# First attention of a two-layer transformer: the correction product in four column strips, and a block's normalization factors on GpSimd

## The chip, the cores and the metric

The kernel runs on one core of a Trainium2 chip. The metric is the device time of one execution in microseconds (us), as the median of several runs. The engines of the core work side by side, each through its own queue in order: TensorE (PE in the profile; its weight loads are PEld), VectorE (DVE), ScalarE (ACT), GpSimd (POOL), and SyncE (SP), which issues most transfers.

## The reference

An image tokenizer gives 128 images of 64 tokens with 256 features. Two layers follow, each with an attention and a feed-forward part, both behind a layer norm and added to the stream. Only the first attention of layer 0 is touched:

```python
h = h + _L0_attn_ref(_layernorm(h), Wq, Wk, Wv, w_mlp, b_mlp)

# in _L0_attn_ref: 8 groups g of 32 features d
Q, K, V = x @ Wq.T, x @ Wk.T, x @ Wv.T
diff = Q[b, q, g, d] - K[b, k, g, d]              # for every pair of tokens q, k
attn = relu(einsum('bqkgd,d->bqkg', relu(diff), w_mlp) + b_mlp[0])
attn = softmax(attn, axis=k)
out  = einsum('bqkg,bkdg->bqdg', attn, V)

# _layernorm(h): (h - mean) / sqrt(var + 1e-5), over the 256 features
```

There is no product of Q and K here: for every pair of tokens and every feature a rectified difference is formed, and only the weighting with `w_mlp` is a matrix product. So VectorE, GpSimd and ScalarE do the elementwise work and TensorE the sums.

## The kernel before

The program has stages one after another: the tokenizer (to about 186 us), the first attention (to about 1102 us), the expert attention of layer 0, the linear attention of layer 1, and the routed experts. The stream `h2` stays in on-chip memory, all in float32.

**Blocks and chunks.** `relu_attention` takes the 128 images in 8 blocks of 16 (`NB`). A block's pairs of query and key are done in 8 chunks of 8 query tokens each, so there are 64 chunks. One chunk's scores lie in one PSUM tile `sc` of 128 partitions (16 images by 8 groups) by 8 queries by 64 keys.

**A chunk's elementwise parts.** For each image `i` and half `hf` of the features a part of 128 x 512 is formed, in one of three ways: `larger` (L530, VectorE) writes max(q, k) in place of relu(q - k), which differs from it by k; `difference` (L538, GpSimd, then L539, ScalarE) writes relu(q - k); `by_query` (L548, ScalarE) does the same for single images. `add` brings the parts of four images into `sc` with `summed` (L340): four products with 32 columns of weights each, which write partitions 0, 32, 64 and 96 onwards. Such four are called a quad here.

**The correction.** Since `larger` gives max(q, k) = relu(q - k) + k, the weighted sum of the keys has to be taken off again. `key_sums` and `correction` (L454) put it, with the bias, into `kb` (128 x 64), once in a block. `begin` spreads it over the 8 queries of a chunk as the first product into `sc` (L525): identity times `kb`, repeated eight times along the free axis.

**The scores after that.** `less_max` (L564 to L566, VectorE), `exponents` (L571, ScalarE), `sums` (L574, L575, VectorE), `weights` (L578, GpSimd), `transpose` (L587, TensorE) and `transposed` (L595, ScalarE) form the softmax of chunk n within chunk n + 1.

**The order.** The order of each engine is written out by hand under `tc.manual_schedule()`. In a chunk TensorE takes six quads of `add`, of which `add(4, 1)` is the last, then the next chunk's `begin`, then the old chunk's `transpose`, and then `add(12, 0)` and `add(12, 1)`, which end the chunk's scores. Steps of the neighbouring blocks are hung into named places of a chunk by the table `work`: "W" lies behind `weights`, ahead of the last differences; "V1" and "V2" lie among VectorE's maxima.

**The factors of a block.** Each block needs its layer norm. `statistics` (L360, L361, VectorE) gives mean and variance for each of 8 tiles (`mv`), `factors` the reciprocal root: L370 adds the epsilon on VectorE, L371 takes the power on GpSimd, both at "W". One chunk later, at "V1", `offsets` (L375, VectorE) multiplies the mean by the factor and by -1. `normal` (L388, ScalarE; L386, VectorE, in the first block alone) applies factor and offset, and transposes and the products for keys, values and queries follow (L397, L409, L428, L463). From block 3 on, four tiles are done at chunk n - 17 and four at n - 13, where n is the block's first chunk.

Of the kernel before, what the change touches and what calls it, by code (L numbers as in the profile page):

```python
# [15 lines left out]
ALU = mybir.AluOpType  # L16
# [4 lines left out]
P = 128  # L21
# [3 lines left out]
LN_EPS = 1e-5  # L25
# [34 lines left out]
def bcast(ap, axis, n):  # L60

    v = ap.unsqueeze(axis)
    shape = list(v.shape)
    shape[axis] = n
    return v.to_broadcast(shape)
# [241 lines left out]
def relu_attention(c, sh, wqkv, wmlp, bmlp, beside):  # L307
# [6 lines left out]
    tc, nc, h2 = c.tc, c.nc, c.h2  # L314
    NB = 16
    NP = NB // 2
    np_, bp, atp, ep = sh.np_, sh.bp, sh.atp, sh.ep
    with (
# [29 lines left out]
        class Block:  # L348
# [14 lines left out]
            def factors(self, i0=0, i1=NP):  # L363

                if i0 == 0:
                    self.rs = np_.tile([P, NP], F32, tag="rs", name="rs")
                    self.nb = np_.tile([P, NP], F32, tag="nb", name="nb")
                i = slice(i0, i1)
                rs = self.rs[:, i]
                nc.vector.tensor_scalar_add(rs, self.mv[:, i, 1], LN_EPS)  # L370
                nc.gpsimd.tensor_tensor(rs, rs, c.nhalf[:, i], ALU.pow)  # L371

            def offsets(self, i0=0, i1=NP):
                i = slice(i0, i1)
                nc.vector.scalar_tensor_tensor(  # L375
                    self.nb[:, i], self.mv[:, i, 0], -1.0, self.rs[:, i], ALU.mult, ALU.mult
                )

            def normal(self, n, vector=False):
                if n == 0:  # L380
# [133 lines left out]
        class Chunk:  # L514
# [7 lines left out]

            def begin(self):
                self.sc = pss.tile([P, 8, T], F32, tag="sc", name="sc")
                nc.tensor.matmul(self.sc, c.ident, bcast(self.blk.kb, 1, 8), start=True, stop=False)  # L525

            def larger(self, pool, i, n, hf):
                m = pool.tile([P, n, 8, T], F32, tag="m", name="m")
# [72 lines left out]
        def at(n, place, *steps):  # L601
            work.setdefault((n, place), []).extend(steps)

        def of(f, *a):
            return lambda: f(*a)

        def first(x):

            for half in range(2):
                for n in range(4 * half, 4 * half + 4):  # L610
                    x.statistics(n)
                x.factors(4 * half, 4 * half + 4)
            for half in range(2):
                x.offsets(4 * half, 4 * half + 4)
            for n in range(4):
                x.normal(n)
                x.normal(4 + n, True)
            for i in (0, 2, 1, 3):
                x.transpose(i)
                x.transposed(i, i > 1)  # L620
            for s in range(2):
                x.keys(s, 0)
                x.keyed(s, 0, s == 1)
            x.queries(0)
            x.queried(0)
# [8 lines left out]
        for b, x in enumerate(blocks):  # L634
            n = 8 * b

            if b + 1 < len(blocks):
                at(n + 9, "X", of(x.outcome, 0))
                at(n + 9, "A", of(x.outcome_copied, 0, 0))
                at(n + 9, "B", of(x.outcome_copied, 0, 1))  # L640
                at(n + 9, "Y", of(x.outcome, 1))
                at(n + 9, "C", of(x.outcome_copied, 1, 0))
                at(n + 10, "O", of(x.outcome_copied, 1, 1))
                for i in range(4):
                    at(n + 10 + i // 2, "XY"[i % 2], of(x.back, i))
                    at(n + 10 + (i + 1) // 2, ("V2", "V1")[i % 2], of(x.added, i))
            if b == 0:
                for i in range(4):
                    at(i // 2 * 2, "XY"[i % 2], of(x.values, i))
                    at(i // 2 * 2, "AB"[i % 2], of(x.valued, i))  # L650
                continue

            if b == 1:
                at(0, "V1", *(of(x.statistics, i) for i in range(NP)))
                at(0, "W", x.factors)
                at(0, "V2", x.offsets)
                at(0, "C", of(x.normal, 0), of(x.normal, 1))
                at(1, "X", of(x.transpose, 0))
                at(1, "A", of(x.normal, 2), of(x.transposed, 0))
                at(1, "B", of(x.normal, 3))  # L660
                at(1, "Z", of(x.transpose, 1))
                at(2, "O", of(x.transposed, 1))
            else:
                for i in range(NP):
                    at(n - 21 + i if b > 2 else 1 + i // 4, "V2", of(x.statistics, i))
                at(n - 17 if b > 2 else 2, "W", of(x.factors, 0, 4))
                at(n - 16 if b > 2 else 3, "V1", of(x.offsets, 0, 4))
                at(n - 13, "W", of(x.factors, 4, 8))
                at(n - 12, "V1", of(x.offsets, 4, 8))
                for i in range(4):  # L670
                    at(n - 12 + i, "C", of(x.normal, i))
                at(n - 8, "X", of(x.transpose, 0))
                at(n - 8, "A", of(x.transposed, 0))
                at(n - 8, "Z", of(x.transpose, 1))
                at(n - 7, "O", of(x.transposed, 1))
            for i in range(2):
                at(n - 6 + i, "A", of(x.normal, 4 + 2 * i))
                at(n - 6 + i, "B", of(x.normal, 5 + 2 * i))
                at(n - 6 + i, "Z", of(x.transpose, 2 + i))
                at(n - 5 + i, "O", of(x.transposed, 2 + i))  # L680
            for fo in range(2):
                at(n - 4 + fo, "X", of(x.keys, 0, fo))
                at(n - 4 + fo, "A", of(x.keyed, 0, fo))
                at(n - 4 + fo, "Z", of(x.keys, 1, fo))
                at(n - 3 + fo, "O", of(x.keyed, 1, fo))
            at(n - 2, "X", of(x.values, 0))
            at(n - 2, "A", of(x.valued, 0))
            at(n - 2, "Y", x.key_sums)
            at(n - 1, "V1", x.correction)
            at(n - 1, "X", of(x.values, 1))  # L690
            at(n - 1, "A", of(x.valued, 1))
            at(n - 1, "Z", of(x.values, 2))
            at(n, "O", of(x.valued, 2))
            at(n, "Y", of(x.values, 3))
            at(n, "B", of(x.valued, 3))
# [8 lines left out]
        with tc.manual_schedule():  # L704
            seq = [(x, q0) for x in blocks for q0 in range(0, T, 8)]
            first(blocks[0])
            ch, old = Chunk(*seq[0]), None
            for n in range(len(seq)):
# [1460 lines left out]
@with_exitstack  # L2169
def vit_tower(ctx: ExitStack, tc: tile.TileContext, a, out):  # L2170
    const = ctx.enter_context(tc.tile_pool(name="const", bufs=1))
    dram = ctx.enter_context(tc.tile_pool(name="dram", bufs=1, space=DRAM))
    c = Ctx(tc, const)

    hd = dram.tile([B, T, D], F32, name="hd")

    hx = dram.tile([B, T, D], F32, name="hx")
    gfd = dram.tile([B * T, 1], F32, name="gfd")
    with tc.tile_pool(name="stream", bufs=1) as sp:
        c.h2 = sp.tile([P, B // 2, D], F32, name="h2")  # L2180
        tokenizer(c, a["x"], a["w1"], a["bn1"], a["w2"], a["bn2"])
        with ExitStack() as rings:
            sh = Shared(c, rings)
            beside, rest = expert_attention(
                c, sh, hd, *(a[k] for k in ("normw", "wr", "br", "wqkvf", "wvf", "wproj", "bproj", "wout"))
            )
            rest(*relu_attention(c, sh, a["wqkv0"], a["wmlp"], a["bmlp"], beside))
    c.tables(ctx.enter_context(tc.tile_pool(name="tables", bufs=1)))
    with tc.tile_pool(name="gate", bufs=1) as gp:
        k = Routing(c, gp, a["wg"], a["bg"])  # L2190
        linear_attention(c, hd, hx, out, k, a["wqk1"], a["bqk1"], a["wv1"], a["bv1"], a["wg"])
        experts(c, hx, gfd, out, a["we1"], a["we2"], a["be2"], lambda: route(c, k, gfd))
# [71 lines left out]
```

## Time and profile before

| What | Value |
|---|---|
| Median of 3 runs | 2685.99 us (2681.73 to 2687.66) |
| The profiled execution | 2687.57 us |
| Its span, first to last instruction | 2685.8 us |
| First attention, in the span | 196 to 1102 us |
| L525, begin: records, between | 128, 201.7 and 1082.9 us |
| L340 into `sc`: records, mean | 4096, 598 ns |
| L375: count, shortest, median, longest | 15; 156, 930, 1866 ns |
| L370: count, median | 15; 118 ns |
| L371: count, median | 15; 1009 ns |
| Granted TensorE clock, mean | 0.981 |

A line of the profile names engine, source line, operation, the tile written and those read, the shape, the count and times. One product in float32 appears as two records of TensorE, so 64 products of `begin` are 128 records. Matmuls are pipelined[...]; how long a product holds the engine is read from the starts of the lines that follow each other. "[0.34 <-DVE m L530]" says that the engine stood idle for 0.34 us and that VectorE's L530 ended the wait.

### The profile page before, as it was taken

Reading aid. Unit: us, or ns where it says so; the run is one execution under the profiler, and the core shown is the slowest. Engines: PE = TensorE matmul, PEld = TensorE weight load, DVE = VectorE, ACT = ScalarE, POOL = GpSimd, SP = SyncE. Lnnn points to the kernel's source line nnn. Section 1 sums busy time; section 2 is a strip of 40 time slices with the busy share of each in tenths; the row PEclk is TensorE's granted clock in tenths of the full one; section 3 lists DMA queues with packets and bytes.
Section 4 is the critical chain, followed back from the end, with each engine's and each line's share of the span. In section 5 each row is a group of like instructions: output and inputs, shape, how many; then the busy total and the mean of one; then the engine's idle time right before and its main releaser. Section 6 shows DMA issues by size and latency. Waiting matters only on the chain.

```text
span 2685.8 us, 80910 instructions
## 1 busy us (share of the span) xinstructions
PE 2539.0 (95%) x35229; PEld 1724.6 (64%) x35229; DVE 2024.2 (75%) x3028; ACT 1624.6 (60%) x3421; POOL 1618.6 (60%) x1381
## 2 busy tenths in 40 slices
PE   8989999999999999899999999999799987999997
PEld 4553444444444444688888888888466565888886
DVE  5759999999999989878877888877367786444443
ACT  2228888888888988766666666665245533332332
POOL 3318889888898998566666666653232312445544
PEclk9999999999999999999999999999899998999998
DMA  3100000000000000000000000000435454555554
GB/s 111 32 13 1 2 2 2 1 2 1 2 2 1 2 12 2 3 12 19 11 11 19 12 19 12 11 19 11 118 64 126 95 123 151 177 193 191 197 186 134
DMA packets 138271, 141.14 MB, mean 53 GB/s; under 512 B 107875, under 2 KB 121701, under 8 KB 130224
## 3 DMA queue, kind: packets, MB, share of 16 engines
q1 hardware_dynamic: 127536, 118.40, 14.8%
q0 software_dynamic: 7648, 14.77, 1.7%
q8 instruction: 278, 4.55, 0.7%
q10 hardware_dynamic: 2720, 2.69, 0.3%
q14 instruction: 89, 0.73, 0.1%
HBM read 104.03 MB, written 32.54 MB: 51 GB/s over the span
## 4 chain that ended last, share of the span: by engine, by line
PE 71%; DVE 18%; issue 4%; ACT 4%; POOL 1%; DMA 1%; DVEq 0%; POOLq 0%; SPq 0%; ACTq 0%
PE sc L340 12%; PE po L2108 6%; DVE m L530 6%; PE ph L2092 6%; PE pc L184 5%; PE pt L1102 4%; PE pqk L1019 4%; PE sc L1066 4%; PE pq L1426 4%; PE pv L1041 3%; PE pz L1115 3%; PE pt L587 2%; PE sc L525 2%; PE pv L1440 2%; PE pk L409 2%
## 5 line engine op out<-in xcount | busy, mean ns | idle before, releaser
L538 POOL TENSOR_TENSOR m<-q,k 128x1024 f32<-128x1024 f32 x384 | 720.1, 1906 | 69.3 <-PE sc L340 56.3
L530 DVE TENSOR_TENSOR m<-pc,k 128x2048 f32<-128x2048 f32 (+1 forms) x320 | 647.2, 2058 | 0.5 <-ACT q L474 0.5
L340 PE MATMUL sc<-m,wide 128*32 128x512 f32 x4096 | 517.3, 598 | 13.9 <-DVE m L530 7.9
L539 ACT ACTIVATE m<-m 128x1024 f32<-128x1024 f32 x384 | 403.0, 1050 | 11.1 <-POOL m L538 10.5
L340 PEld LDWEIGHTS sc<-m,wide 128*32 128x32 f32 x4096 | 127.8, 109 | 281.4 <-issue 165.7
L548 ACT ACTIVATE m<-k,q 128x64 f32<-128x64 f32 x1024 | 271.0, 340 | 0.9 <-DVE k L421 0.9
L1078 DVE TENSOR_REDUCE mx<-sc 128x16 f32<-128x1024 f32 x128 | 156.1, 1220 | 135.3 <-PE sc L1066 135.3
L1093 POOL TENSOR_TENSOR e<-e,mx 128x1024 f32<-128x1024 f32 x128 | 243.6, 1903 | 10.0
L1025 ACT COPY kr<-pqk 128x512 f32<-128x512 f32 x254 | 137.7, 603 | 140.4 <-PE pqk L1019 140.4
L2092 PE MATMUL ph<-xt,w1s 128*128 128x256 f32 x896 | 198.9, 380 | 3.6 <-DVE xt L2083 2.7
L2108 PE MATMUL po<-w2s,hT 128*128 128x256 f32 x896 | 198.0, 379 | 0.0
L1092 POOL TENSOR_TENSOR mx<-mx,gate 128x16 f32<-128x16 f32 x128 | 27.7, 216 | 278.9 <-ACT z L1123 152.7
L2092 PEld LDWEIGHTS ph<-xt,w1s 128*128 128x128 f32 x896 | 169.8, 190 | 28.3 <-DVE xt L2083 3.3
L2108 PEld LDWEIGHTS po<-w2s,hT 128*128 128x128 f32 x896 | 168.1, 190 | 21.7
L1105 ACT COPY pT<-pt 128x512 f32<-128x512 f32 x256 | 139.0, 598 | 50.4 <-PE pt L1102 50.0
L1079 DVE TENSOR_TENSOR e<-sc,mx 128x1024 f32<-128x1024 f32 x128 | 156.7, 1225 | 4.4
L2126 POOL DMA_INDIRECT out<-y,rout x56 | 56.8, 1013 | 167.7 <-ACT hT L2096 124.8
L1085 DVE TENSOR_REDUCE mx<-e 128x16 f32<-128x1024 f32 x128 | 152.5, 1191 | 4.0 <-ACT e L1082 3.8
L1102 PE MATMUL pt<-ident,e 128*128 128x128 f32 x1024 | 143.1, 282 | 9.5 <-DVE vr L1055 6.3
L2096 ACT ACTIVATE hT<-ph,w1s 128x256 f32<-128x256 f32 x224 | 93.2, 471 | 96.8 <-PE ph L2092 96.8
L2113 ACT ACTIVATE y<-y,gf 128x256 f32<-128x256 f32 x56 | 28.0, 507 | 196.4 <-issue 107.3
L1082 ACT ACTIVATE e<-e 128x1024 f32<-128x1024 f32 x128 | 139.5, 1090 | 2.2 <-DVE e L1079 1.9
(330 smaller groups left out, 5013.6 us busy)
## 6 DMA issues: line engine op xcount, KB each, us to landing
w1s<-in_we SPq DMA_DIRECT2D x30, 1028.0 KB, 5.2
w2s<-in_we SPq DMA_DIRECT2D x30, 1024.0 KB, 4.9
hd<-h SPq DMA_DIRECT2D x16, 512.0 KB, 3.4
x<-hd SPq DMA_DIRECT2D x16, 512.0 KB, 3.9
h<-hd SPq DMA_DIRECT2D x4, 2048.0 KB, 12.8
hx<-h SPq DMA_DIRECT2D x4, 2048.0 KB, 11.8
out<-h SPq DMA_DIRECT2D x4, 2048.0 KB, 20.6
xt<-in_x SPq DMA_DIRECT2D x15, 512.0 KB, 3.6
```

The source lines that it names most:

```text
L340: nc.tensor.matmul(dst[j : j + 32], wide[:, hf, s : s + 32], part, start=start, stop=stop)
L530: nc.vector.tensor_tensor(m, bcast(self.pq[:, hf, i : i + n], 3, T), k, ALU.max)
L538: nc.gpsimd.tensor_tensor(m, bcast(self.q[:, hf, s : s + 2], 3, T), k, ALU.subtract)
L539: nc.scalar.activation(m, m, AF.Relu)
L548: nc.scalar.activation(self.parts[i, hf][:, q], self.blk.k[:, hf, i], AF.Relu, bias=self.q[:, hf, i - NB // 2, q : q + 1], scale=-1.0,)
L1078: nc.vector.tensor_reduce(mx, sc, AX.X, ALU.max)
L1079: nc.vector.tensor_sub(e, sc, bcast(mx, 2, T))
L1085: nc.vector.tensor_reduce(self.sm[x], self.e[x], AX.X, ALU.add)
L1093: nc.gpsimd.tensor_mul(e, e, bcast(sm, 2, T))
L1102: nc.tensor.transpose(pt[:, cq, :], e[:, i : i + 2, :].rearrange("p e s -> p (e s)"), c.ident)
L2092: nc.tensor.matmul(ph[:, j], self.w1[:, w0 : w0 + P], self.xt[:, fc], start=(fc == 0), stop=(fc == 1))
L2108: nc.tensor.matmul(po, self.hT[:, f, r * P : r * P + P], self.w2[:, f, :], start=(f == 0), stop=(f == 7))
```

## The change

`begin` forms the same sum in four products: 32 columns of the identity at a time, each into its 32 partitions of `sc`, with the same moving operand. `factors` does all its steps on GpSimd: the epsilon, the power, and then the offset in two steps, mean times factor and times -1. `offsets` and its places in the table are gone, so the offsets are formed at "W", one chunk before, and in the first block half by half. What is computed stays the same.

```diff
@@ factors, offsets
-                nc.vector.tensor_scalar_add(rs, self.mv[:, i, 1], LN_EPS)
+                nc.gpsimd.tensor_scalar_add(rs, self.mv[:, i, 1], LN_EPS)
                 nc.gpsimd.tensor_tensor(rs, rs, c.nhalf[:, i], ALU.pow)
-
-            def offsets(self, i0=0, i1=NP):
-                i = slice(i0, i1)
-                nc.vector.scalar_tensor_tensor(
-                    self.nb[:, i], self.mv[:, i, 0], -1.0, self.rs[:, i], ALU.mult, ALU.mult
-                )
+                nc.gpsimd.tensor_mul(self.nb[:, i], self.mv[:, i, 0], rs)
+                nc.gpsimd.tensor_scalar(self.nb[:, i], self.nb[:, i], -1.0, None, ALU.mult)
@@ begin
-                nc.tensor.matmul(self.sc, c.ident, bcast(self.blk.kb, 1, 8), start=True, stop=False)
+                for j in range(0, P, 32):
+                    j = slice(j, j + 32)
+                    nc.tensor.matmul(
+                        self.sc[j], c.ident[:, j], bcast(self.blk.kb, 1, 8), start=True, stop=False
+                    )
@@ first
-            for half in range(2):
-                x.offsets(4 * half, 4 * half + 4)
@@ the table of steps
                 at(0, "W", x.factors)
-                at(0, "V2", x.offsets)
...
                 at(n - 17 if b > 2 else 2, "W", of(x.factors, 0, 4))
-                at(n - 16 if b > 2 else 3, "V1", of(x.offsets, 0, 4))
                 at(n - 13, "W", of(x.factors, 4, 8))
-                at(n - 12, "V1", of(x.offsets, 4, 8))
```

## The prediction

> **What bounds the kernel now.** I read the page first, then the stretches of the span, then the chain of waits, and then the order of time around the two places that change. The profiled execution took 2687.57 us, span 2685.8; it lies 1.6 above the median of the runs, 2685.99.
>
> ```profile
> PE 2539.0 (95%) x35229; PEld 1724.6 (64%) x35229; DVE 2024.2 (75%) x3028; ACT 1624.6 (60%) x3421; POOL 1618.6 (60%) x1381
> ...
> PE 71%; DVE 18%; issue 4%; ACT 4%; POOL 1%; DMA 1%; DVEq 0%; POOLq 0%; SPq 0%; ACTq 0%
> ```
>
> TensorE (PE) carries the span, VectorE (DVE) the rest. The change lies in the first attention, 196 to 1102 us; its stretch (busy us of PE, PEld, DVE, ACT and POOL, with instructions; then clock, DMA share, GB/s), and the chain in it by line:
>
> ```profile
> 196.00:1102.00 906.00, 891.42 (x9599) 392.51 (x9598) 851.15 (x849) 788.74 (x1781) 804.39 (x486) 1.00 0.01 2
> ```
> ```profile
> by line: PE sc L340 35.4%; DVE m L530 17.8%; PE pt L587 6.4%; PE sc L525 6.1%; PE pk L409 5.0%; PE pc L463 4.9%; PE pv L428 4.8%; PE po L484 2.2%; DVE e L566 1.8%; DVE pc L564 1.8%; ACT m L539 1.7%; DVE mx L574 1.5%; DVE nb L375 1.4%; DVE h
> ```
>
> PE is busy 98% and DVE 94%, and the chain goes to and fro between them. Both lines that change stand in it: PE L525 with 6.1% of 906 = 55.3 us, DVE L375 with 1.4% = 12.7 us. GpSimd (POOL) is busy 89% but hardly in the chain.
>
> PE in order of time (start, duration, count of records; each fp32 product has two records). Starts tell more than durations, which overlap:
>
> ```profile
> 606.61 1.07 PE L340 MATMUL sc<-m,wide 128*32 128x512 f32 x8 [0.32 <-DVE m L530]
> 607.61 1.13 PE L525 MATMUL sc<-kb,ident 128*128 128x512 f32 x2
> 608.66 1.15 PE L587 MATMUL pt<-ident,e 128*64 128x64 f32 x32
> 609.75 1.98 PE L409 MATMUL pk<-xT,w 128*128 128x512 f32 x4
> ...
> 626.10 2.78 PE L340 MATMUL sc<-m,wide 128*32 128x512 f32 x24
> 628.81 1.99 PE L428 MATMUL pv<-w,xT 128*128 128x256 f32 x8
> ```
>
> One quad of column strips (8 records) takes 607.61 - 606.61 = 1.00 us to the next line, three quads (24) take 628.81 - 626.10 = 2.71. So a further quad costs (2.71 - 1.00)/2 = 0.857, and leaving the strip shape 0.14. The full-array product L525 takes 608.66 - 607.61 = 1.05; four such records (L409, next line at 611.66) take 1.91, so a product costs 0.86 and leaving the full shape 0.20. **A quad costs what one full product costs; the rest is the price of changing shape.**
>
> **What the Trainium skill says.** TensorEngine Tiling (Array Packing), Key Properties: a change of tiling mode, not of the tile alone, drains TensorE, and different tiles run in parallel. The trace agrees: 0.14 and 0.20 at changes, and four strips in the time of one product. SBUF — State Buffer, Who interferes with whom: a DVE instruction with two SBUF inputs contends with a GpSimd instruction that reads SBUF, and the later one blocks fully. The trace agrees at L375 (inputs `mv` and `rs`): 0.16 us at the start, where POOL is idle, but 0.93 as median:
>
> ```profile
> L375 DVE SCALAR_TENSOR_TENSOR nb<-mv,rs x15: 156/930/1866, 186.3 to 826.2; 128x4 f32<-128x4 f32 x14, 128x8 f32<-128x8 f32 x1
> ```
>
> **Part 1, begin.** One 128-column product becomes four 32-column ones. They follow `add(4, 1)`, which is in the strip shape already, so quad, begin, leave costs 2 x 0.857 + 0.14 = 1.85 where it was 1.00 + 1.05 = 2.05. Gain 0.197 us for each of 64 chunks. The first product keeps the wait of L525 (for `kb`, or for the strips before); the other three have none. On the chain stand 55.3 / 1.055 = 52 of 64: **52 x 0.197 = 10.2 us**. The other 12 lie where DVE is late anyway; nothing there. Unshown: that four strips may read the same moving operand (`kb`) at full rate; in L340 each strip has its own. Bounds: -12.6 (all 64 count) to the rival below; I take 10.2.
>
> **Part 2, DVE's steps go.** L370 (15, 0.12 us) and L375 leave DVE; between 196 and 1102 there are 13 of each. L370 adds 0.03 from start to start: 0.3 us in all. L375 comes twice in a block of eight chunks:
>
> ```profile
> 432.58 1.36 DVE L375 SCALAR_TENSOR_TENSOR nb<-mv,rs 128x4 f32<-128x4 f32 x1
> 433.87 2.28 DVE L530 TENSOR_TENSOR m<-pc,k 128x2048 f32<-128x2048 f32 x1
> ...
> 488.43 0.53 DVE L375 SCALAR_TENSOR_TENSOR nb<-mv,rs 128x4 f32<-128x4 f32 x1
> 488.88 2.28 DVE L530 TENSOR_TENSOR m<-pc,k 128x2048 f32<-128x2048 f32 x1
> ```
> ```profile
> 436.92 1.92 PE L340 MATMUL sc<-m,wide 128*32 128x512 f32 x16
> 439.18 1.07 PE L340 MATMUL sc<-m,wide 128*32 128x512 f32 x8 [0.34 <-DVE m L530]
> ...
> 491.00 2.87 PE L340 MATMUL sc<-m,wide 128*32 128x512 f32 x16
> 494.19 1.06 PE L340 MATMUL sc<-m,wide 128*32 128x512 f32 x8 [0.32 <-DVE m L530]
> ```
>
> The first holds DVE 1.29 us, the second 0.45. Both are followed by PE waiting for DVE's last maximum, and the gain ends when PE waits no more. Two quads take 1.71: at 439.18 PE is 439.18 - 436.92 - 1.71 = 0.55 late, at 494.19 it is 1.48. So 0.55 of the 1.29 counts and all of 0.45; PE is next. Five blocks: 5 x (0.55 + 0.45) = 5.0. Three lie outside that pattern: at 826.22 it holds DVE 1.79 and PE waits longer than that for the next maximum, so 1.8; at 262.32 1.7, with PE 1.48 late: 1.5; at 248.63 0.85, all of it. Sum with L370: **9.4 us**; below, half of it (4.7), if the 0.55 and 0.45 are cut by Part 1; above, the chain's 12.7 + 0.6.
>
> **Part 3, POOL's steps come.** L370 and two more land at each of 15 places, behind the weights (L578), ahead of the last difference L538. Prices by GpSimd rows of this size:
>
> ```profile
> 888.60 0.20 POOL L904 TENSOR_TENSOR mr<-mv,rs 128x4 f32<-128x4 f32 x1
> 888.88 0.20 POOL L905 TENSOR_TENSOR rs<-rs,one 128x4 f32<-128x4 f32 x1
> ```
>
> From start to start 0.28, so 3 x 0.28 = 0.85 us each, 13 x 0.85 = 11 us in this stretch, where POOL idles over 90. Behind them wait `difference(14, 0)`, ACT's relu (L539), then PE:
>
> ```profile
> 481.52 1.06 ACT L539 ACTIVATE m<-m 128x1024 f32<-128x1024 f32 x1 [0.20 <-POOL m L538]
> ```
>
> It ends at 482.58, PE reads it from 483.43: 0.85 of slack. With Part 1, PE comes 0.2 earlier and waits about 0.2; but it is 1.48 late at 494.19 anyway, so nothing is lost there. In the other such chunk of a block the slack is 2.6. I take 1.5 us lost for all; bounds 0 and 13 x 0.85 = 11. ACT's next copies have idle time ahead of them (0.4 and 1.1 us). No DMA moves and no queue but POOL's is passed.
>
> **The start.** The chain passes L370 and L375 at 186.19 and 186.26; the first half's offsets now come at about 185.8 instead of 186.4, the second half's 0.2 later. From -0.6 to +0.4; I take 0.
>
> **Sum.** -10.2 - 9.4 + 1.5 = -18.1, that is 2687.6 - 18.1 = 2669.5 against the profiled time and 2686.0 - 18 = 2668 against the median. Behind 1102 us nothing is touched; that work comes earlier.
>
> **The rivals.**
> 1. *Only PE gains* (begins shorten; PE, now the bound, or POOL's 11 us eat DVE's gain): -10, 2676. For it: PE at 98%. Against: PE visibly waits 1.48 at 494.19. Chance 0.14.
> 2. *Only DVE gains*: the price at a change of shape is one of each new product, so the merge saves nothing: -9.4 + 1.5, 2678. Against: quads inside a run follow each other at 0.857. Chance 0.10.
> 3. *Slower: strips that share `kb` run one after another.* Begin then costs 4 x 0.857 = 3.43 for 0.857: 64 x (3.43 - 1.05) = +152, 2830. It decides the sign once begin takes 1.055 + 8/52 = 1.2 us. For it: no row shows a shared moving operand. Against: the strips of L340 read four operands without loss. Chance 0.04.
> 4. *Nothing gained*: both gains meet a wait for ACT (87%) or POOL: 2686. Chance 0.06. The change does what it says: the changed program's order has four 32x512 products for the one, and 30 DVE instructions fewer.
>
> **How the numbers follow.** Forecast 0.66 (2660 to 2674: all of 12.6 + 13.3, or a third less). It and the first two rivals hold the range 2659 to 2680. What can be told from no change is 0.2%, 5.4 us: faster below 2680.6. Faster 0.89, same 0.06, slower 0.05.
>
> **What would show it.** Begin's line with 512 records, and 1.85 us from the start of the quad ahead of it to the line behind it, where 2.05 passed; no small DVE steps between L566 and L530; PE late by about 0 at the first place and 1.0 to 1.2 at the second; the stretch near 888 us instead of 906. Wrong if begin's four strips start over 0.1 us apart, if PE's wait for ACT L539 grows by over 5 us, or if stages behind 1102 change in length.

## The result, and the profile after

The kernel after takes 2667.24 us as the median of five runs (2664.47 to 2671.78), the kernel before 2685.99: 18.8 us less, a ratio of 0.9935 with a 95% interval of 0.9923 to 0.9948. The forecast was 2668. Nearly all of it lies in the first attention. From the first statistics (L360) to the end of the last L566, called the stage from here on, 921.0 us pass before and 902.8 after, 18.2 less; the sum in the prediction was 18.1. What follows the stage takes 1583.2 us before and 1583.7 after. The part ahead of it, which the change does not touch, took 181.6 us in the profile of before and 179.1 in that of after, so the two profiled executions lie somewhat further apart.

The page after, engines and chain:

```profile
PE 2523.5 (95%) x35613; PEld 1729.0 (65%) x35613; DVE 2009.8 (75%) x2998; ACT 1621.5 (61%) x3421; POOL 1627.9 (61%) x1426
...
PE 75%; DVE 13%; issue 5%; ACT 4%; POOL 2%; DMA 1%; SPq 0%; POOLq 0%; DVEq 0%; ACTq 0%
```

The stretch of the stage (length, then busy us of PE, PEld, DVE, ACT and POOL):

```profile
196.00:1083.00 887.00, 877.07 (x10071) 397.14 (x10072) 836.58 (x823) 787.90 (x1783) 811.86 (x525) 1.00 0.01 3
```

The chain in that stretch by line:

```profile
by line: PE sc L340 45.9%; PE pt L587 7.1%; DVE m L530 7.0%; PE pc L459 6.6%; PE pk L405 6.1%; PE pv L424 5.9%; PE sc L523 5.8%; PE po L480 2.2%; ACT m L539 2.2%; PE pt L393 1.6%; ACT m L548 1.1%; PE pto L498 0.9%; issue 0.9%; DVE e L566 0.
```

VectorE's share of the chain has fallen: L530 from 17.8% to 7.0%, and L375 is gone. TensorE is now the bound nearly everywhere, which is why L340 rises from 35% to 46% though it does the same work. GpSimd has 9 us more to do.

TensorE in order of time, at the first and then at the second of a block's two places:

```profile
429.51 2.78 PE L340 MATMUL sc<-m,wide 128*32 128x512 f32 x24
432.11 1.04 PE L523 MATMUL sc<-kb,ident 128*32 128x512 f32 x8
433.08 1.15 PE L587 MATMUL pt<-ident,e 128*64 128x64 f32 x32
434.16 0.66 PE L393 MATMUL pt<-ident,xn 128*128 128x128 f32 x4
...
482.71 3.49 PE L340 MATMUL sc<-m,wide 128*32 128x512 f32 x24
486.02 1.04 PE L523 MATMUL sc<-kb,ident 128*32 128x512 f32 x8
486.99 1.15 PE L587 MATMUL pt<-ident,e 128*64 128x64 f32 x32
```

Three quads lead to begin in 432.11 - 429.51 = 2.60 us (2.71 led to another shape before), begin to the transpose in 0.97 (1.05 before). Three quads are 2.57, so at the first place TensorE is 0.03 late for VectorE's maximum, where it was 0.55; at the second it is 486.02 - 482.71 - 2.57 = 0.74 late, where it was 1.48.

GpSimd at the second place:

```profile
470.19 0.23 POOL L370 TENSOR_SCALAR rs<-mv 128x4 f32<-128x4 f32 x1
470.49 1.04 POOL L371 TENSOR_TENSOR rs<-rs,nhalf 128x4 f32<-128x4 f32 x1
471.61 0.20 POOL L372 TENSOR_TENSOR nb<-mv,rs 128x4 f32<-128x4 f32 x1
471.90 0.24 POOL L373 TENSOR_SCALAR nb<-nb 128x4 f32<-128x4 f32 x1
472.09 7.50 POOL L538 TENSOR_TENSOR m<-q,k 128x1024 f32<-128x1024 f32 x4
```

From L370 to the next difference 1.90 us pass; L371 alone took 0.98 from start to start before. With a start that is 0.13 later this makes the difference 1.06 us late, not 0.85. L371 now takes 1.12 from start to start: L372, which reads its result, starts 0.08 us after its end, where the difference, which does not, started 0.03 before it. Why L370 starts later behind L578 than L371 did is not known.

### The profile page after: what moved, and what is told of

It is laid out like the page before. It is cut to its first block, busy times and chain, and to the rows that moved or that the text cites. A ratio compares the mean times of both kernels' runs of the same rounds, so it can differ in the third digit from the quotient of the medians.

```text
span 2665.5 us, 81705 instructions
## 1 busy us (share of the span) xinstructions
PE 2523.5 (95%) x35613; PEld 1729.0 (65%) x35613; DVE 2009.8 (75%) x2998; ACT 1621.5 (61%) x3421; POOL 1627.9 (61%) x1426
## 4 chain that ended last, share of the span: by engine, by line
PE 75%; DVE 13%; issue 5%; ACT 4%; POOL 2%; DMA 1%; SPq 0%; POOLq 0%; DVEq 0%; ACTq 0%
PE sc L340 15%; PE po L2103 6%; PE ph L2087 6%; PE pc L184 5%; PE pt L1097 4%; PE sc L1061 4%; PE pqk L1014 4%; PE pq L1421 4%; PE pv L1036 3%; PE pz L1110 3%; PE pt L587 2%; DVE m L530 2%; PE pc L459 2%; PE pk L405 2%; DVE mx L1073 2%
## 5 line engine op out<-in xcount | busy, mean ns | idle before, releaser
L538 POOL TENSOR_TENSOR m<-q,k 128x1024 f32<-128x1024 f32 x384 | 719.7, 1907 | 56.4 <-PE sc L340 44.5
L530 DVE TENSOR_TENSOR m<-pc,k 128x2048 f32<-128x2048 f32 (+1 forms) x320 | 646.4, 2056 | 0.5 <-ACT q L470 0.5
L340 PE MATMUL sc<-m,wide 128*32 128x512 f32 x4096 | 517.1, 597 | 8.5 <-ACT m L539 6.2
L539 ACT ACTIVATE m<-m 128x1024 f32<-128x1024 f32 x384 | 403.1, 1051 | 21.3 <-POOL m L538 21.3
L340 PEld LDWEIGHTS sc<-m,wide 128*32 128x32 f32 x4096 | 130.9, 109 | 270.1 <-issue 159.4
```

The costliest lines, as they stand in the source:

```text
L340: nc.tensor.matmul(dst[j : j + 32], wide[:, hf, s : s + 32], part, start=start, stop=stop)
L530: nc.vector.tensor_tensor(m, bcast(self.pq[:, hf, i : i + n], 3, T), k, ALU.max)
L538: nc.gpsimd.tensor_tensor(m, bcast(self.q[:, hf, s : s + 2], 3, T), k, ALU.subtract)
L539: nc.scalar.activation(m, m, AF.Relu)
```

## The experiments

All stage times are of the profiled executions. The second to the fifth block are called steady: in before they take 112.42 us each, and in most of the kernels below they repeat to 0.02 us (to 0.14 in `e6_pool_more` and `e8_x_by_queries`; `e3_halves` has an idle spell in one of them).

**Each part alone.** `e1_strips` is before with the four strips of begin and nothing else; `e2_factors` is after with

```diff
-                for j in range(0, P, 32): ...
+                nc.tensor.matmul(self.sc, c.ident, bcast(self.blk.kb, 1, 8), start=True, stop=False)
```

> The kernel before with begin alone in four strips; factors and offsets stay on VectorE. The first attention (first statistics to the end of the last L566) lasts 921.0 us before and 902.8 after. My theory, that each begin on the chain saves the one price of leaving the full shape: 52 x 0.197 = 10.2 us less, so about 911 us and a median near 2676. Rival (the price belongs to each new product, and all of the gain is VectorE's): 921, no change.

> The kernel before with the factors and offsets alone on GpSimd; begin stays one full product. My theory: 9.4 us less from VectorE, 1.5 lost to GpSimd's steps, so 913 us for the stage and a median near 2678; it and the strips then add up to the whole change. Rival (PE alone bounds the stage): under 2 us less.

The strips alone: stage 910.6, 10.4 less, median 2672.4 (ratio 0.9956, 0.9941 to 0.9970). The factors alone: 912.2, 8.8 less, median 2676.3 (0.9971, 0.9959 to 0.9982). Both parts gain, each by about what was forecast (10.2, and 9.4 - 1.5 = 7.9). In a steady block of eight chunks the strips gain 1.38 us, the factors 1.00, and the kernel after 2.36: the parts add up. Over the stage 10.4 + 8.8 is 1.0 more than 18.2. Of this 0.8 lies ahead of the first begin, which comes 20.2 us after the stage's start in after and 19.4 in `e2_factors`, though both run the same instructions up to there: between 181 and 190 us the granted TensorE clock was 0.50 in the profile of after and 0.62 in that of `e2_factors`. That is scatter, not the change. From the first begin to the last the strips gain 10.6 us, the factors 8.1, and both together 18.6.

**Is it the shape?** `e3_halves` makes begin of two products of 64 columns, the shape of the transpose behind it.

```diff
-                for j in range(0, P, 32):
-                    j = slice(j, j + 32)
+                for j in range(0, P, 64):
+                    j = slice(j, j + 64)
```

> The kernel after, but begin in two products of 64 columns of the identity, the shape of the transpose (L587) that follows, in place of four of 32 columns, the shape of the quad ahead. My theory counts changes of shape alone: there are as many as in the kernel after (quad to begin, not begin to transpose), so the stage lasts 902 to 904 us, and no time lies between begin and L587. Rival (strips of 32 columns are quicker in themselves, or only the quad's own line can be continued): as with the full product, about 912.

TensorE in order of time:

```profile
427.92 2.78 PE L340 MATMUL sc<-m,wide 128*32 128x512 f32 x24
430.63 1.08 PE L523 MATMUL sc<-kb,ident 128*64 128x512 f32 x4
431.54 1.10 PE L587 MATMUL pt<-ident,e 128*64 128x64 f32 x32
432.57 0.66 PE L393 MATMUL pt<-ident,xn 128*128 128x128 f32 x4
...
441.64 0.62 PE L340 MATMUL sc<-m,wide 128*32 128x512 f32 x1
442.80 2.78 PE L340 MATMUL sc<-m,wide 128*32 128x512 f32 x23 [0.55 <-issue]
```

From the quads to the line behind the transpose: 432.57 - 427.92 = 4.65 us, and in the kernel after 434.16 - 429.51 = 4.65. Now the price lies ahead of begin (2.71), and behind it almost none is left (0.91 us to the transpose, where a product costs 0.86). Two shapes with one change between them, in either order, cost the same; the full product had a shape of its own between two others. The stage is 904.4, 0.4 above the range: two idle spells of TensorE of 1.2 and 1.4 us, one of them in the last two lines, end with no wait that the profile shows. Without them it would be 901.9; the first begin comes 0.8 us earlier than in after, by the clock as above. A steady block without such a spell takes 110.05 us, and 110.06 in after. The rival, 912, is out.

**Is it the second input?** `e4_one_input` has the strips, and keeps the offsets on VectorE at their old places:

```diff
-                nc.vector.scalar_tensor_tensor(
-                    self.nb[:, i], self.mv[:, i, 0], -1.0, self.rs[:, i], ALU.mult, ALU.mult
-                )
+                for i in range(i0, i1):
+                    nc.vector.tensor_scalar(
+                        self.nb[:, i : i + 1], self.mv[:, i, 0:1], self.rs[:, i : i + 1], -1.0, ALU.mult, ALU.mult
+                    )
```

> The kernel before with begin in four strips, and the offsets on VectorE at their old places, but as one product per tile, with the factor as a scalar of that tile: one tensor input each in place of two. My theory (two inputs in SBUF make L375 wait for GpSimd's running instruction): each of these takes 0.06 to 0.2 us and none is stretched to 0.5 or more; GpSimd has only the power to do, so the stage lasts 902 to 906 us. Rival (L375 waited for the power's result or its semaphore): some are stretched to 0.5 to 1.9 us as before, and the stage lasts about 911.

The offsets' line (shortest, median, longest in ns):

```profile
L375 DVE TENSOR_SCALAR nb<-mv,rs x64: 200/203/214, 184.4 to 813.7; 128x1 f32<-128x1 f32 x64
```

None of 64 is stretched, at places where the form with two inputs took 0.37 to 1.87 us beside a running L538. The trace of before says the same: each of the 13 stretched L375 began while an L538 ran on GpSimd, and ended about 0.02 us after it, as here at 828.09 and 828.07:

```profile
826.15 1.92 POOL L538 TENSOR_TENSOR m<-q,k 128x1024 f32<-128x1024 f32 x1
826.22 1.87 DVE L375 SCALAR_TENSOR_TENSOR nb<-mv,rs 128x4 f32<-128x4 f32 x1
```

Nor is it the operation: L566 is a SCALAR_TENSOR_TENSOR too, with one of its two inputs in PSUM, and none of 64 is stretched, though GpSimd is busy 89% of the stretch.

```profile
L566 DVE SCALAR_TENSOR_TENSOR e<-sc,mx x64: 691/692/693, 219.2 to 1101.9; 128x512 f32<-128x512 f32 x64
```

So L375 waited for the GpSimd instruction that ran, and not for the power's result. This fits the port that both engines share, as the Trainium skill says in SBUF — State Buffer, Who interferes with whom. That page does not say whether a scalar operand from memory counts as an input; here it does not. The stage is 905.3, the median 2671.6. Against `e1_strips`, from which it differs in the form of the offsets alone, the stage is 5.3 us shorter: so much the second input had cost. Four short rows hold VectorE some 0.5 us, more than no row, so the change as made is better by 2.5.

**What a quad costs.** `e5b_extra_quad` doubles begin's work with weights of zero. They are columns of the table `wide`, because on-chip memory had no room for a tile of their own, which `e5_extra_quad` was to have; that run gave no result:

```diff
+                for j in range(0, P, 32):
+                    j = slice(j, j + 32)
+                    nc.tensor.matmul(self.sc[j], none, bcast(self.blk.kb, 1, 8), start=False, stop=False)
```

> The kernel after with four more strip products behind begin in every chunk, with zero columns of the table wide as weights, so they add nothing to the scores: begin's work once more, in the same shape and with the same shared moving operand. It measures what a quad within a run costs, and which share of TensorE's time turns into time. My theory: 0.857 us for each, 54.9 us of TensorE over 64 chunks; 52 of 64 begins are on the chain, so 44.6 us at least, and up to 54.9 where VectorE's lead is used up: a stage of 947 to 958 us (902.8 after). Rival (the shared moving operand slows the strips): over 1.0 us for each, over 958. Rival (TensorE has slack in many chunks): under 40 us more.

```profile
602.49 1.04 PE L524 MATMUL sc<-kb,ident 128*32 128x512 f32 x8
603.35 1.04 PE L529 MATMUL sc<-kb,wide 128*32 128x512 f32 x8
604.32 1.15 PE L593 MATMUL pt<-ident,e 128*64 128x64 f32 x32
```

The second quad follows after 0.86 us: strips that share a moving operand run side by side at full rate, and the slower rival of the prediction is out. The stage is 949.7, so 46.9 of the 54.9 us turn into time. A steady block grows by 6.00 us, 7 x 0.857: of eight chunks one, where TensorE waited for VectorE, grows by nothing. It is also the one in which the strips gained nothing. Of the 46.9, 1.1 us lie in one chunk of a later block that is longer than its like elsewhere; the runs do not show why.

**GpSimd's cover.** `e6_pool_more` does the two offset steps three times; `e7_later` moves the factors behind the last difference:

```diff
-                at(n - 17 if b > 2 else 2, "W", of(x.factors, 0, 4))
-                at(n - 13, "W", of(x.factors, 4, 8))
+                at(n - 17 if b > 2 else 2, "C", of(x.factors, 0, 4))
+                at(n - 13, "C", of(x.factors, 4, 8))
```

> The kernel after with the two new GpSimd steps of the offsets done three times at each place, four steps more (some 1.1 to 1.2 us). It measures what GpSimd's lateness costs. My theory: in one of the two places of a block it is covered by 2.6 us of slack; in the other TensorE comes later by the full amount, and of that all but the 0.7 us is absorbed that TensorE is late there for VectorE: about 0.5 us a block, 2 to 5 us in all, a stage of 905 to 908. Rival (GpSimd's steps are fully hidden): 903. Rival (they are on the path wherever they are): 13 x 1.2 = 16 us, 918.

> The kernel after with the factors of blocks 2 to 7 at the end of the same chunk (place C, behind the last difference) in place of W, ahead of it. The last difference is then not late for ScalarE and TensorE; the next chunk's first difference is, which has 3 us of slack. My theory: the strips alone gained 10.4 and the factors alone 8.8 us, 1.0 more than both together, and this 1.0 and some of the 1.5 that I had put down for GpSimd is its lateness; so a stage of 900.5 to 902 us. Rival (the shortfall is VectorE and TensorE overlapping, not GpSimd): 902.8, no change.

Both expectations missed. `e7_later`: stage 902.7, median 2668.3 (0.9941, 0.9921 to 0.9962), no change. TensorE is no longer late for GpSimd at the second place, but then it only waits longer for VectorE:

```profile
484.33 3.88 PE L340 MATMUL sc<-m,wide 128*32 128x512 f32 x24
488.02 1.04 PE L523 MATMUL sc<-kb,ident 128*32 128x512 f32 x8
```

488.02 - 484.33 - 2.57 = 1.12 us late in place of 0.74. From begin to begin every chunk of the stage is as long as in after, to 0.01 us. So the late last difference costs nothing in the kernel after. `e6_pool_more`: stage 916.4, 13.6 us more than after, median 2683.1 (ratio to before 1.000, 0.999 to 1.001): 4.6 us of the gain are left in the stage, and nothing that the runs can tell. Its last difference comes 1.19 us later than after's, and in a steady block 0.92 us of that is lost at the first place and 0.98 at the second. The cover that after leaves is thus 0.2 to 0.3 us. (Another 2.0 of the 13.6 lie ahead of the first begin, where all the work waits for the factors.) At the first place it breaks where I had not looked. ScalarE and TensorE in after, early in the next chunk:

```profile
423.49 1.05 ACT L539 ACTIVATE m<-m 128x1024 f32<-128x1024 f32 x1
424.83 1.92 PE L340 MATMUL sc<-m,wide 128*32 128x512 f32 x16
426.69 1.16 PE L459 MATMUL pc<-xT,w 128*128 128x128 f32 x8
```

and the same in `e6_pool_more`, with L540 and L460 for L539 and L459:

```profile
430.18 1.05 ACT L540 ACTIVATE m<-m 128x1024 f32<-128x1024 f32 x1
430.36 2.83 PE L340 MATMUL sc<-m,wide 128*32 128x512 f32 x16
433.13 1.16 PE L460 MATMUL pc<-xT,w 128*128 128x128 f32 x8
```

The late difference itself does not hold TensorE up there. But ScalarE takes its work in order and has no idle time from the late difference's relu to that of `difference(10, 0)`, which is therefore late as well. In after that relu ends at 424.54, and TensorE comes to its quad, `add(8, 0)`, at 424.83: 0.29 us to spare. In `e6_pool_more` it ends at 431.23, 0.87 after TensorE came, and the two quads last 2.77 us in place of 1.86. At the second place TensorE waits for the late difference itself: its chunk is 0.68 us longer, the next one 0.30.

**Fewer changes of shape.** If shape is the price, other steps can be put beside their like. `e8_x_by_queries` moves place X (full products of a neighbouring block) to just ahead of the queries; `e9_z_by_queries` moves four steps from place Z to Y, just behind them. Both start from `e7_later`.

```diff
# e8_x_by_queries
-                do(n, "X")
                 ch.difference(10, 0)
...
+                do(n, "X")
                 if n + 1 < len(seq):
                     seq[n + 1][0].queries(seq[n + 1][1])
# e9_z_by_queries
-                at(n - 8, "Z", of(x.transpose, 1))
+                at(n - 8, "Y", of(x.transpose, 1))
-                at(n - 4 + fo, "Z", of(x.keys, 1, fo))
+                at(n - 4 + fo, "Y", of(x.keys, 1, fo))
-                at(n - 1, "Z", of(x.values, 2))
+                at(n - 1, "Y", of(x.values, 2))
```

> The kernel of e7_later with one more change of order on TensorE: the steps of place X (a neighbouring block's products, full shape in seven chunks of eight) no longer stand between two quads but directly ahead of the queries (L459), which have the full shape too. If changes of shape are what costs, each such chunk has one run of strips and one of full products less, 0.14 + 0.20 = 0.34 us of TensorE, 19 us over 56 chunks, of which the chunks where TensorE waits for VectorE keep nothing: a stage of 886 to 893 us. Rival: ScalarE's copies of X's results, some 3 us later in its order, stall it and the rectified differences behind it, and the stage lasts 903 us or more.

> The kernel of e7_later with four of the six full-shape steps that a block has at place Z (transpose(1), the second halves of the keys, values(2)) moved to place Y, right behind the queries (L459), which have the full shape. Their results are copied only at the start of the next chunk, so ScalarE's order stays as it was, other than with place X. Shape theory: one leaving of the full shape less, 0.20 us, in each of 27 chunks, 5.4 us of TensorE, some of it where TensorE waits for VectorE anyway: a stage of 898 to 901 us, against 902.7. Rival (products moved ahead of add(8, 1) delay the chunk's later quads and the engines that wait for them, or hold a PSUM buffer too long): 903 or more.

`e8_x_by_queries` is slower: stage 942.8, median 2706.3 (1.0085, 1.0068 to 1.0102). Its waits:

```profile
PEld sc L340 <- ACT m L539: 86.8, 105, 2.1
...
ACT v L435 <- PE pv L424: 15.8, 19, 2.3
...
ACT k L417 <- PE pk L405: 11.5, 16, 1.5
```

In `e7_later`, from which it starts, the last two were 4.0 and 0.4, the first 38.7: ScalarE reaches its copies before the products are there, stands, and the rectified differences behind the copies hold TensorE. `e9_z_by_queries` leaves ScalarE its order and gains: stage 897.0, median 2662.8, ratio to before 0.9918 (0.9905 to 0.9932), the lowest of all. The interval overlaps that of after (0.9923 to 0.9948), so the gain is read from the stage.

```profile
480.52 1.16 PE L459 MATMUL pc<-xT,w 128*128 128x128 f32 x8
481.51 1.88 PE L405 MATMUL pk<-xT,w 128*128 128x512 f32 x4
483.32 2.78 PE L340 MATMUL sc<-m,wide 128*32 128x512 f32 x24
...
486.89 1.15 PE L587 MATMUL pt<-ident,e 128*64 128x64 f32 x32
487.98 2.78 PE L340 MATMUL sc<-m,wide 128*32 128x512 f32 x24
```

The keys follow the queries after 0.99 us, where a line of another shape comes after 1.09, and take 1.81 in place of 1.92: 0.21 together. The transpose leads straight to the quads. Of the 5.7 us against `e7_later` 0.8 lie ahead of the first begin, the clock's scatter as above; 4.9 us are left for 27 moves of 0.20 each, 5.4 in all. A steady block, with four moves, takes 109.25 us in place of 110.05. The keys' weights are not those of the queries, and yet the price falls: it goes with the change of shape, not with new weights.

## Why the prediction was right

- **Begin, 10.2 us: held.** 10.4 measured alone, 1.38 a steady block, which is 7 x 0.197. The prediction's 52 of 64 would be 6.5 of 8, so its share was a little low, but counting the begins on the chain and not all 64 was the right step: all 64 would give 12.6.
- **VectorE's steps, 9.4 us: right at most places, too high in sum.** From begin to begin `e2_factors` gains 0.54 us in the chunk of a first place, 0.45 in that of a second and 1.79 in that of 826.22, where 0.55, 0.45 and 1.8 were said: the step from what VectorE gives up to what TensorE stops waiting for was right. But at 248.63 and 262.32 it gains 0.5 and 1.2, where 0.85 and 1.5 were said. And the list of places was misread: of the five second places that it counts, only four hold 0.45; the fifth is the one at 826.22, counted once more. The thirteenth step, at 213.56 us, held VectorE 0.29 and was left out.
- **GpSimd's steps, 1.5 us lost: mis-sized.** The late last difference costs 0 (`e7_later`), though the delay was underpriced, 1.06 us for 0.85. And the sentence "In the other such chunk of a block the slack is 2.6" names the wrong slack: it is TensorE's for that one difference; the differences behind it in ScalarE's queue have far less. That the delay costs nothing is in part luck: the true slack there, some 1.3 us (1.06 and the 0.27 of the 1.19 that `e6_pool_more` did not lose), was just enough.
- **The sum came out better than its terms.** With GpSimd's loss at 0, VectorE's term was too high by about as much as GpSimd's was: 9.4 - 1.5 = 7.9 was forecast for the two, and 8.1 measured from the first begin to the last. That these errors cancel is luck.
- **The marks.** Begin's four strips start within 0.02 us. The first place came out as said (0.03 late). At the second 1.0 to 1.2 was forecast, 0.74 measured, and `e7_later`, without GpSimd's delay, shows 1.12. The mark set for failure, TensorE's wait for L539 up by over 5 us, was passed (43.0 to 48.7 for loads and products together) and still the sum held. In `e7_later` that wait is 45.3 and the chunks are as long, so it was a poor mark.
- **The start, taken as 0:** from the stage's start the first transposes come 0.45 us earlier than before, the first keys 0.37 later and the first begin 0.15 later, within the bounds.

## What to carry to other kernels

Price a product of TensorE with the shape of its neighbours in the queue: here equal work cost 0.20 us less where it continued the shape ahead of it or behind it, and moving like beside like gained again, as long as no engine in order then waits for the moved result. An instruction of VectorE with two inputs in memory beside a busy GpSimd is worth moving or rewriting when its line's median lies far above its shortest. And when work is put on an engine with idle time, look for the slack in the queues of the engines that it feeds, not only at the one consumer that is named.

## What was not expected of the hardware

Leaving the shape of 128 x 32 strips costs less (0.14 us) than leaving the full one (0.20). GpSimd's steps of 4 columns take 0.20 to 0.25 us each (the power 1.04), and short ones that the next step waits for start 0.29 to 0.31 us ahead of it; in before, L910, which touches other columns than L905 ahead of it, started 0.15 us after it (889.03 and 888.88). A scalar operand of VectorE, read from memory, did not bring on the wait for GpSimd that a second tensor input does (64 of 64 at 0.20 to 0.21 us).
